# The last four tiles' norms and queries of layer 1 made in rounds of its blocks, and the first gate chain in steps within the feed-forward

## The chip, the cores and the metric

The kernel runs on one core of a Trainium2 chip. The metric is device time in microseconds (us), the median of the runs shown. The engines are named as in the profile: PE is TensorE (PEld its weight loads), DVE is VectorE, ACT is ScalarE, POOL is GpSimd, SP is the queue from which most transfers are issued.

## The reference

Two layers run on 2048 rows of 512 numbers; each layer is an attention over a fixed context and a feed-forward, each with a residual. The part that matters here is the end of layer 0 and the beginning of layer 1:

```python
# layer 0, feed-forward: every activation rounded to 8 bits by row, weights to -1, 0, 1
h = silu(bitlinear(n, w1)) * bitlinear(n, w3)          # n = layernorm(x), 1408 columns
x = x + bitlinear(h, w2)
# layer 1, attention (an mLSTM in parallel form), 8 batches of 256 rows, 16 heads of 32
q  = layernorm(x)
ig = concat(q, ctx, ctx) @ Wi + bi                     # gates, one number for each row and head
fg = concat(q, ctx, ctx) @ Wf + bf
F  = cumsum(log_sigmoid(fg))                           # over the 256 rows
log_D[s, t] = F[s] - F[t] + ig[t]                      # for t <= s
D  = exp(log_D - max_t log_D)
C  = (q @ ctx.T) / sqrt(32) * D
h  = C / (max(|sum_t C|, exp(-max_t log_D)) + 1e-6) @ ctx
x  = x + headwise_norm(h) * ln_scale
# layer 1, feed-forward: 32 experts, 4 for each row, and one shared expert
```

## The kernel before, in words

The 2048 rows are 16 tiles of 128 rows (0 to 15), held in SBUF as `g.X`.

**The feed-forward of layer 0** (`layer0_ffn`) is a software pipeline over tiles. For tile i: `ffn_input` normalizes it on ACT (`xn`), `quantize` takes the row maximum on DVE (`am`), rounds on ACT (line 407) and clips on DVE (`xq`, line 408). `xqT` is that tile transposed by a DMA from the SP queue. `hidden` runs 24 products on PE with w1 and w3 (`p`, line 556), in three chunks of columns; each chunk has an ACT instruction (`sg`, the silu) and a DVE instruction (`h`). The 1408 columns are then rounded in the same manner (`am`, ACT line 407, `hq`), and `hqT` is transposed by a DMA. `output` runs 11 products (`py`, line 575), and DVE adds the result to the tile (`x`, line 576). Two tiles' hidden products can be in flight, since `p1` and `p3` have two PSUM buffers each. The order of instructions on each engine is made here by a scheduler, from the order of the program.

Behind the output, `front(i)` takes the tile's mean and variance for layer 1 (`st`, `mv`). For groups of tiles (0 to 3, 4 to 7, 8 to 11, 12 to 14, and 15 alone) DVE computes the inverse square roots (`rsqrt`, lines 88 to 93, dependent instructions on 128x4 numbers) and `nb`. Each tile is then normalized on ACT, transposed on PE (`ft`, line 584) and copied by ACT to `qT` (`turned`). These pieces wait in the list `todo`, from which two are taken in each step.

**The gates** (class `Gates`). `context` and `queries` sum the gates of all rows in one PSUM tile `pg`; `kept(h)` copies half of it to SBUF (`gs`). `chain(h, ...)` is a generator with one `yield` a step: PE sorts the gates (`gates`, line 502), then bias (DVE, 507 and 508), log-sigmoid (ACT, 511 to 513, with table loads), cumulative sum and maximum (DVE, 515 to 519), then six bf16 parts of two rows of numbers (lines 527 and 529, "casts" and "subtractions" below), each sent to DRAM (`parts_d`), and `em`. Half 0 serves batches 0 to 3, half 1 batches 4 to 7. Half 0 needs tiles 0 to 7 alone. Its chain is begun at the last step but two, so that it runs behind the last tiles.

**The attention of layer 1** (`layer1_attention`). First the constants: `left` is cleared on POOL, `right` is filled on DVE (lines 692, 693, 695), and both get rows from `parts_d` by DMA (`values`). Then 32 blocks (8 batches by 4 groups of heads) run in rounds, in an order written by hand on PE, ACT, DVE and POOL. In round n: the decays of block n (`pd` on PE, lines 726 and 727; `xe`, exponentials on ACT, line 731), the weights of block n-1 (`pqk` on PE, `ct` on DVE, line 754), the products of block n-2 (`num`, line 767, and its copy `numT` on ACT, line 775), and `back` of block n-3. `tail` does the norms of a batch later on. From round 3 on each round takes one step of the second gate chain (half 1), whose PSUM tiles come from the tag `pqk`, of two buffers.

Of the kernel before, what the change touches and what calls it, by code (L numbers as in the profile page):

```python
# [19 lines left out]
F32 = mybir.dt.float32  # L20
BF16 = mybir.dt.bfloat16
# [3 lines left out]
AF = mybir.ActivationFunctionType  # L25
ALU = mybir.AluOpType
# [370 lines left out]
def quantize(g, out, tmp, x):  # L397


    nc = g.nc  # L400
    am = g.small.tile([P, 1], F32, tag="am", name="am")
    nc.vector.tensor_reduce(am, x, AX.X, ALU.max, apply_absolute_value=True)
    inv = g.small.tile([P, 1], F32, tag="qi", name="qi")
    nc.vector.tensor_scalar(inv, am, 1e-5, 1.0 / 127.0, ALU.max, ALU.mult)
    sc = g.small.tile([P, 1], F32, tag="qs", name="qs")
    nc.vector.reciprocal(sc, inv)
    nc.scalar.activation(tmp, x, AF.Identity, bias=g.eps["magic"], scale=sc)
    nc.vector.tensor_scalar(out, tmp, MAGIC, 127.0, ALU.subtract, ALU.min)
    return inv


def ffn_input(g, work, i):

    nc = g.nc
    if i in (0, 4):
        of = slice(0, 4) if i == 0 else slice(4, NT)
        nc.scalar.activation(g.rs[:, of], g.mv[:, of, 1], AF.Sqrt, bias=g.eps["ln"])
        nc.vector.reciprocal(g.rs[:, of], g.rs[:, of])
        nc.vector.scalar_tensor_tensor(g.mv[:, of, 0], g.mv[:, of, 0], -1.0, g.rs[:, of], ALU.mult, ALU.mult)
    xn = work.tile([P, D], F32, tag="y", name="xn")  # L420
    nc.scalar.activation(xn, g.X[i], AF.Identity, bias=g.mv[:, i, 0:1], scale=g.rs[:, i : i + 1])
    xq = work.tile([P, D], BF16, tag="xq", name="xq")
    ix = quantize(g, xq, xn, xn)
    s13 = g.fin.tile([P, 2], F32, tag="s13", name="s13", bufs=4)
    nc.vector.tensor_scalar(s13, g.iw[:, :2], ix, None, ALU.mult)
    return xq, s13
# [9 lines left out]
class Gates:  # L436
# [4 lines left out]
    def __init__(self, g, wp):  # L441
# [12 lines left out]
        self.parts = [wp.tile([P, S], BF16, tag=f"part{n}", name=f"part{n}") for n in range(3)]  # L454
# [4 lines left out]
        self.fg, self.af, self.ig, self.F, self.gg, self.M = (row() for _ in range(6))  # L459

# [10 lines left out]
    def context(self, ps):  # L471

        self.pg = ps.tile([P, CH], F32, tag="pg", name="pg", bufs=1)
        for k in range(KD):
            for c in range(NCH):
                self.g.nc.tensor.matmul(
                    self.pg[c * 2 * H1 : (c + 1) * 2 * H1, :], lhsT=self.Wkv[:, k, :], rhs=self.g.ctxT[c][:, k, :],
                    start=k == 0, stop=False,
                )

    def queries(self, chunks, cols=slice(0, CH)):

        for k in range(KD):
            for c in chunks:
                self.g.nc.tensor.matmul(
                    self.pg[c * 2 * H1 : (c + 1) * 2 * H1, cols], lhsT=self.W[:, k, :], rhs=self.g.qT[c][:, k, cols],
                    start=False, stop=k == KD - 1 and cols.stop == CH,
                )

# [4 lines left out]
    def chain(self, h, two, turned):  # L494
# [11 lines left out]
        yield  # L506
        nc.vector.tensor_scalar(fg, both[r, 1], self.bif[r, 1:2], None, ALU.add)
        nc.vector.tensor_scalar(ig, both[r, 0], self.bif[r, 0:1], None, ALU.add)
# [14 lines left out]
        yield  # L523

        for n, rest in enumerate((gg, M)):
            for m, part in enumerate(self.parts):
                nc.vector.tensor_copy(part[r], rest)
                if m < 2:
                    nc.vector.tensor_sub(rest, rest, part[r])
                (nc.sync if n or h else nc.scalar).dma_start(out=g.parts_d[n, m, r], in_=part[r])  # L530
            yield
# [3 lines left out]
        yield  # L535
        em = self.em[:, :, r]
        nc.scalar.activation(em, pm[:, :, r], AF.Exp, scale=-1.0)

# [3 lines left out]
def layer0_ffn(g, tc, gates):  # L542
# [4 lines left out]
    with tc.tile_pool(name="f0work", bufs=2, reuse_waits="tile") as work, tc.tile_pool(name="f0ps", bufs=2, space=PSUM, reuse_waits="tile") as ps:  # L547

        def hidden(i, xqT, s1, s3):
# [15 lines left out]
            ih = quantize(g, hq, h, h)  # L565
            s2 = work.tile([P, 1], F32, tag="s2", name="s2", bufs=4)
            nc.vector.tensor_mul(s2, ih, g.iw[:, 2:3])
            hqT = work.tile([P, NF, P], BF16, tag="hqT", name="hqT", bufs=3)
            nc.sync.dma_start_transpose(out=hqT, in_=hq)
            return hqT, s2  # L570
# [19 lines left out]
        groups = {3: range(4), 7: range(4, 8), 11: range(8, 12), 14: range(12, 15), 15: range(15, 16)}  # L590
        mv = {}
        todo = []

        def front(i):
            if i == 0:
                todo.append(partial(gates.context, ps))
            for first, of in ((of[0], of) for of in groups.values()):
                if i in of:
                    if i == first:
                        mv["now"] = work.tile([P, 4, 2], F32, tag="mv4", name="mv4")  # L600
                    norm_stats(g, mv["now"][:, i - first, :], g.X[i])
            if i in groups:
                of = groups[i]
                m = mv["now"]
                var = work.tile([P, 4], F32, tag="var4", name="var4")
                nc.vector.tensor_scalar(var[:, : len(of)], m[:, : len(of), 1], 1e-5, None, ALU.add)
                *_, rs = rsqrt(g, var[:, : len(of)], len(of))
                nb = work.tile([P, 4], F32, tag="nb4", name="nb4")
                nc.vector.scalar_tensor_tensor(nb[:, : len(of)], m[:, : len(of), 0], -1.0, rs, ALU.mult, ALU.mult)
                for n, t in enumerate(of):  # L610
                    todo.append(partial(turned, t, rs[:, n : n + 1], nb[:, n : n + 1]))
                    if t == 7:
                        todo.append(partial(gates.queries, (0, 1)))
                        todo.append(partial(gates.kept, 0))
                    if t == 11:
                        todo.append(partial(gates.queries, (2,)))
                    if t > 11:
                        todo.append(partial(gates.queries, (3,), slice((t - 12) * P, (t - 11) * P)))
# [3 lines left out]
        for n in range(len(xq), NT + 5):  # L622
            if n >= 5:
                output(n - 5, *hq.pop(n - 5))
            if 0 <= n - 2 < NT:
                hq[n - 2] = hidden(n - 2, *xq.pop(n - 2))
            if n >= 5:
                front(n - 5)
            for _ in range(2):
                if todo:  # L630
                    todo.pop(0)()
            if n < NT:
                xq[n] = ffn_turned(g, *ffn_input(g, work, n))
            if n == NT + 1:
                one = lambda: ps.tile([P, 2, S], F32, tag="ft", name="gates", bufs=1)
                first = gates.chain(0, one, one)
                for _ in range(8):
                    next(first)
        while todo:
            todo.pop(0)()  # L640
        gates.kept(1)
        for _ in first:
            pass
# [31 lines left out]
def layer1_attention(g, tc, gates):  # L675
    nc = g.nc
    with ExitStack() as ctx:
# [10 lines left out]
        for l, r in zip(left, right):  # L688
            nc.gpsimd.memset(l, 0.0)
            nc.gpsimd.memset(l[:KR], 1.0)  # L690
            if r is right[0]:
                nc.vector.tensor_copy(r[:, 0], g.head.unsqueeze(2).to_broadcast([P, HG, S]))
                nc.vector.tensor_copy(r[:, 1:], r[:, :1].to_broadcast([P, KD - 1, HG, S]))
            else:
                nc.vector.tensor_copy(r, right[0])

        with tc.tile_pool(name="a1ps2", bufs=1, space=PSUM, reuse_waits="tile") as ps, tc.tile_pool(name="a1work", bufs=2, reuse_waits="tile") as work:
            def values(b):

                V = []  # L700
                for j in range(2):
                    v = work.tile([P, D], F32, tag=f"raw{j}", name=f"raw{j}")
                    nc.sync.dma_start(out=v, in_=g.vc_d[b * S + j * P : b * S + (j + 1) * P, :])
                    V.append(v)
# [8 lines left out]
                )  # L713
                return V

# [140 lines left out]
            V, hid, xe, ct, num, numT = {0: values(0)}, {}, {}, {}, {}, {}  # L856
# [4 lines left out]
            def tail(n, r0):  # L861
# [41 lines left out]
            second = gates.chain(  # L903
                1, lambda: ps.tile([P, 2, CH], F32, tag="pqk", name="gates", bufs=2)[:, :, :S],
                lambda: ps.tile([P, 2, CH], F32, tag="pqk", name="pmT", bufs=2)[:, :, :P],
            )

            def round_(n):
# [4 lines left out]
                if 0 <= n - 3 < len(blocks):  # L913
                    b, k = blocks[n - 3]
                    if k == 0:
                        hid[b] = work.tile([P, 2, H1, HD1 + 1], F32, tag="hid", name="hid", bufs=3)
                    back(numT.pop(n - 3), hid[b], k)
# [11 lines left out]
                if n >= 3:  # L929
                    next(second, None)  # L930
# [575 lines left out]
```

## Time and profile before

| | |
|---|---|
| median of 5 runs | 1148.17 us (1145.92 to 1153.21) |
| the profiled execution: its time, its span | 1145.78 us, 1144.0 us |
| mean granted clock of PE | 0.971 |
| PE, DVE, ACT, POOL busy, share of the span | 90%, 48%, 36%, 33% |
| feed-forward of layer 0: first and last product with w1 or w3 | 239.0 and 371.0 us |
| attention of layer 1: first decay product, last `numT` | 407.3 and 557.9 us |

Times inside the execution are counted from the start of its span. A timeline line has start, duration, engine, line, operation, `out<-in`, shapes, how many instructions were merged, and in brackets the engine's idle time just before with what ended it. Lines "SPq" are issues of transfers, not the transfers themselves. In a window line the columns are the window, its length, and for PE, PEld, DVE, ACT, POOL the busy time and the number of instructions, then the granted PE clock, the share of the DMA engines and GB/s.

### The profile page before, as it was taken

Reading aid. Unit: us, or ns where it says so; the run is one execution under the profiler, and the core shown is the slowest. Engines: PE = TensorE matmul, PEld = TensorE weight load, DVE = VectorE, ACT = ScalarE, POOL = GpSimd, SP = SyncE. Lnnn points to the kernel's source line nnn. Section 1 sums busy time; section 2 is a strip of 40 time slices with the busy share of each in tenths; the row PEclk is TensorE's granted clock in tenths of the full one; section 3 lists DMA queues with packets and bytes.
Section 4 is the critical chain, followed back from the end, with each engine's and each line's share of the span. In section 5 each row is a group of like instructions: output and inputs, shape, how many; then the busy total and the mean of one; then the engine's idle time right before and its main releaser. Section 6 shows DMA issues by size and latency. Waiting matters only on the chain.

```text
span 1144.0 us, 14676 instructions
## 1 busy us (share of the span) xinstructions
PE 1034.0 (90%) x5222; PEld 617.1 (54%) x5222; DVE 547.2 (48%) x1443; ACT 412.3 (36%) x701; POOL 375.8 (33%) x347
## 2 busy tenths in 40 slices
PE   7989799989899688898898989999999999999994
PEld 5746466534444255555443445555556665667672
DVE  6545645568888636988845951121221211221210
ACT  4445424155675357578541002111122222111111
POOL 0144522220000001354651033444454555444422
PEclk9999899999999799899899989999999999999997
DMA  9786311023323111221022345766777777788872
GB/s 343 262 284 209 125 56 46 5 50 61 61 52 65 41 40 41 66 78 57 37 92 65 138 149 149 184 167 185 179 193 191 196 197 198 211 226 231 221 186 35
DMA packets 100483, 153.65 MB, mean 134 GB/s; under 512 B 38600, under 2 KB 41288, under 8 KB 100376
## 3 DMA queue, kind: packets, MB, share of 16 engines
q1 hardware_dynamic: 81488, 106.94, 30.2%
q0 software_dynamic: 18672, 45.58, 18.1%
q8 instruction: 43, 0.70, 0.3%
q14 instruction: 40, 0.33, 0.1%
q10 hardware_dynamic: 240, 0.10, 0.0%
HBM read 111.24 MB, written 33.49 MB: 127 GB/s over the span
## 4 chain that ended last, share of the span: by engine, by line
PE 55%; DMA 12%; DVE 11%; issue 7%; ACT 6%; POOL 6%; SPq 0%; POOLq 0%; DVEq 0%; ACTq 0%
PE po L1270 10%; PE pg L1254 9%; PE pu L1254 8%; PE p L556 3%; PE pz L371 3%; PE pw L316 3%; DMA xg<-h_d,tok_of 3%; DMA out_x<-eo,to 2%; POOL out_x L1314 2%; DMA hqT<-hq 2%; PE pt L1310 2%; DMA vc_d<-raw 2%; DMA raw<-in_ctx 2%; DVE xT L1311 2%; ACT xe L731 1%
## 5 line engine op out<-in xcount | busy, mean ns | idle before, releaser
L1314 POOL DMA_INDIRECT out_x<-eo,to x84 | 129.8, 1545 | 226.5 <-ACT eo L1340 211.6
L1254 PE MATMUL pg<-xT,w 128*128 128x288 f32 (+7 forms) x512 | 140.3, 417 | 3.9 <-DVE xT L1311 3.9
L1270 PE MATMUL po<-w,act 128*128 128x512 f32 (+3 forms) x448 | 139.4, 494 | 4.1 <-DVE act L1259 3.8
L1254 PE MATMUL pu<-xT,w 128*128 128x288 f32 (+7 forms) x512 | 136.7, 410 | 0.0
L1258 ACT ACTIVATE sg<-pg 128x288 f32<-128x288 f32 (+8 forms) x68 | 28.9, 425 | 257.6 <-PE pg L1254 254.1
L1340 ACT ACTIVATE eo<-po,slotw 128x512 f32<-128x512 f32 (+3 forms) x112 | 64.2, 578 | 158.8 <-PE po L1270 156.5
L1254 PEld LDWEIGHTS pg<-xT,w 128*128 128x128 f32 x512 | 95.4, 191 | 33.8 <-DVE xT L1311 7.3
L1254 PEld LDWEIGHTS pu<-xT,w 128*128 128x128 f32 x512 | 97.2, 190 | 29.1 <-issue 3.0
L1311 DVE COPY xT<-pt 128x512 f32<-128x512 f32 (+3 forms) x84 | 48.9, 619 | 132.2 <-PE pt L1310 132.1
L1305 DVE SCALAR_TENSOR_TENSOR of<-xg,is_rank 128x32 f32<-128x32 f32 (+3 forms) x84 | 15.8, 188 | 187.2 <-DMA xg<-h_d,tok_of 186.0
L1295 POOL DMA_INDIRECT xg<-h_d,tok_of x84 | 82.6, 983 | 65.0 <-DVE act L1259 37.1
L1270 PEld LDWEIGHTS po<-w,act 128*128 128x128 f32 (+3 forms) x448 | 55.7, 161 | 79.2 <-issue 49.4
L556 PE MATMUL p<-wq,xqT 128*128 128x512 bf16 (+1 forms) x384 | 79.7, 362 | 2.7 <-DMA xqT<-xq 1.9
L754 DVE SCALAR_TENSOR_TENSOR ct<-pqk,xe 128x768 f32<-128x768 f32 x64 | 58.3, 950 | 26.6 <-ACT xe L731 12.9
L316 PE MATMUL pw<-wg,xnT 128*128 128x512 f32 x128 | 60.6, 618 | 0.0
L556 PEld LDWEIGHTS <-xqT 128*128 128x128 bf16 x384 | 36.7, 98 | 44.1 <-DMA xqT<-xq 6.3
L371 PE MATMUL pz<-wo,wyT 128*128 128x512 f32 x128 | 57.9, 595 | 1.5 <-ACT wyT L365 1.5
L1310 PE MATMUL pt<-ident,xg 128*128 128x128 f32 (+4 forms) x336 | 46.1, 269 | 11.7 <-DVE xT L1311 11.7
L731 ACT ACTIVATE xe<-pd 128x512 f32<-128x512 f32 x96 | 54.0, 598 | 5.4 <-PE pd L727 5.0
L1259 DVE TENSOR_TENSOR act<-pu,sg 128x288 f32<-128x288 f32 (+8 forms) x68 | 32.1, 475 | 44.4 <-PE pu L1254 44.1
L1310 PEld LDWEIGHTS pt<-ident,xg 128*128 128x128 f32 (+4 forms) x336 | 35.0, 140 | 31.4 <-DVE xT L1311 16.5
L812 POOL TENSOR_TENSOR hid<-hid,rsq 128x1024 f32<-128x1024 f32 x8 | 15.3, 1913 | 105.5 <-PE pqk L750 79.3
(287 smaller groups left out, 1707.7 us busy)
## 6 DMA issues: line engine op xcount, KB each, us to landing
w<-in_w SPq DMA_DIRECT2D x32, 1024.0 KB
w<-in_w SPq DMA_DIRECT2D x32, 512.0 KB
wst<-in_w1T SPq DMA_DIRECT2D x8, 704.0 KB
wst<-in_w3T SPq DMA_DIRECT2D x8, 704.0 KB
wst<-in_w2T SPq DMA_DIRECT2D x6, 768.0 KB
x<-in_x SPq DMA_DIRECT2D x16, 256.0 KB
ctxT<-in_ctxT_d SPq DMA_DIRECT2D x4, 1024.0 KB
raw<-in_ctx SPq DMA_DIRECT2D x16, 256.0 KB
```

What stands on the lines that cost most here:

```text
L316: nc.tensor.matmul(pw, lhsT=xnT[c][:, k, o : o + P], rhs=wg[:, k, :], start=k == 0, stop=k == KD - 1)
L371: nc.tensor.matmul(pz, lhsT=wyT[:, k, :], rhs=wo[:, k, :], start=k == 0, stop=k == KD - 1)
L556: nc.tensor.matmul(pp[:, : z - a], lhsT=xqT[:, k, :], rhs=w[:, k, a:z], start=k == 0, stop=k == KD - 1)
L731: nc.scalar.activation(out, pd, AF.Exp)
L754: nc.vector.scalar_tensor_tensor(ct[:, r : r + 2, :], pqk[:, :, : S + P], 1.0 / math.sqrt(HD1), xe[:, r : r + 2, :], ALU.mult, ALU.mult,)
L1254: nc.tensor.matmul(pp[:, :n], lhsT=w[:, k, cols], rhs=xT[:, k, :n], start=k == 0, stop=k == KD - 1)
L1270: nc.tensor.matmul(po[h * n : (h + 1) * n, :cols], lhsT=act[:, m, j * P : j * P + n], rhs=w[:, m, h * cols : (h + 1) * cols], start=m == 0 ...
L1295: nc.gpsimd.indirect_dma_start(out=xg[:n], out_offset=None, in_=h_d, in_offset=bass.IndirectOffsetOnAxis(ap=g.tok_of[:n, r, j : j + 1], ax ...
L1310: nc.tensor.transpose(pt[:, k, :n], xg[:n, k * P : (k + 1) * P], g.ident[:n, :n])
L1311: nc.vector.tensor_copy(xT, pt[:, :, :n])
L1314: return nc.gpsimd.indirect_dma_start(out=g.out, out_offset=bass.IndirectOffsetOnAxis(ap=rows, axis=0), in_=eo, in_offset=None, compute_op ...
L1340: nc.scalar.activation(eo[:n, at : at + cols], po, AF.Copy, scale=w[:n, j : j + 1])
```

## The change

Tiles 12 to 15 are no longer normalized, transposed and multiplied into the gates at the end of the feed-forward. Their means and variances go to a tile that outlives it (`gates.last`), one set of inverse square roots for all four is made at the start of `layer1_attention` (`norm_scales`), and the function `extra` puts the rest in rounds: `yn` (ACT) in rounds 1 and 2, transposes and `qT` in rounds 2 and 3, the products of chunk 3 with the gate weights in round 4, added to `gs` by DVE.

The first gate chain is taken in steps, two at each of the last three steps of the feed-forward; what is left of it (`em`) falls in rounds 2 and 3. The two bias instructions are on ACT instead of DVE, and the parts have buffers of their own. The second chain begins at round 6 instead of 3, with the PSUM tag `dec` instead of `pqk`. `todo` gives three pieces a step instead of two. For the last four tiles of the feed-forward the order on PE, ACT and DVE is written out: outputs 12, hidden 15 up to the rounding on ACT, outputs 13 and 14 with their statistics, what `todo` still has, then `hq` of tile 15, and output 15. Two of the three copies that fill `right` are on ACT, and `values` issues `left` and `right` ahead of `raw`.

```diff
@@ quantize
-    nc.vector.tensor_scalar(out, tmp, MAGIC, 127.0, ALU.subtract, ALU.min)
-    return inv
+    return inv, lambda: nc.vector.tensor_scalar(out, tmp, MAGIC, 127.0, ALU.subtract, ALU.min)
...
@@ Gates
+    def added(self, pg):
+        rows = slice((NCH - 1) * 2 * H1, NCH * 2 * H1)
+        self.g.nc.vector.tensor_add(self.gs[rows], self.gs[rows], pg[rows])
...
-        yield
-        nc.vector.tensor_scalar(fg, both[r, 1], self.bif[r, 1:2], None, ALU.add)
-        nc.vector.tensor_scalar(ig, both[r, 0], self.bif[r, 0:1], None, ALU.add)
+        nc.scalar.activation(fg, both[r, 1], AF.Identity, bias=self.bif[r, 1:2])
+        nc.scalar.activation(ig, both[r, 0], AF.Identity, bias=self.bif[r, 0:1])
         yield
...
-            for m, part in enumerate(self.parts):
+            for m, part in enumerate(self.parts[n]):
                 nc.vector.tensor_copy(part[r], rest)
                 if m < 2:
                     nc.vector.tensor_sub(rest, rest, part[r])
-                (nc.sync if n or h else nc.scalar).dma_start(out=g.parts_d[n, m, r], in_=part[r])
+                nc.sync.dma_start(out=g.parts_d[n, m, r], in_=part[r])
...
@@ layer0_ffn, hidden
+            yield
+            end()
             nc.sync.dma_start_transpose(out=hqT, in_=hq)
-            return hqT, s2
+            yield hqT, s2
...
@@ layer0_ffn, the steps
+        gates.first = gates.chain(0, one, lambda: gates.turned_in())
+        for n in range(len(xq), NT + 1):
             if n >= 5:
                 output(n - 5, *hq.pop(n - 5))
+            if n >= 2:
+                *_, hq[n - 2] = hidden(n - 2, *xq.pop(n - 2))
             if n >= 5:
                 front(n - 5)
+                for _ in range(3):
+                    if todo:
+                        todo.pop(0)()
+            if n >= NT - 2:
+                for _ in range(2):
+                    next(gates.first)
             if n < NT:
                 xq[n] = ffn_turned(g, *ffn_input(g, work, n))
-            if n == NT + 1:
-                one = lambda: ps.tile([P, 2, S], F32, tag="ft", name="gates", bufs=1)
-                first = gates.chain(0, one, one)
-                for _ in range(8):
-                    next(first)
-        while todo:
-            todo.pop(0)()
-        gates.kept(1)
-        for _ in first:
-            pass
+        with tc.manual_schedule(engines={E_.PE, E_.Activation, E_.DVE}):
+            i = NT - 4
+            output(i, *hq.pop(i))
+            last = hidden(NT - 1, *xq.pop(NT - 1))
+            next(last)
+            front(i)
+            for i in (NT - 3, NT - 2):
+                output(i, *hq.pop(i))
+                front(i)
+            while todo:
+                todo.pop(0)()
+            hq[NT - 1] = next(last)
+            gates.kept(1)
+            output(NT - 1, *hq.pop(NT - 1))
+            front(NT - 1)
...
@@ layer1_attention
-                nc.vector.tensor_copy(r[:, 0], g.head.unsqueeze(2).to_broadcast([P, HG, S]))
-                nc.vector.tensor_copy(r[:, 1:], r[:, :1].to_broadcast([P, KD - 1, HG, S]))
+                nc.scalar.copy(r[:, 0], g.head.unsqueeze(2).to_broadcast([P, HG, S]))
+                nc.scalar.copy(r[:, 1:], r[:, :1].to_broadcast([P, KD - 1, HG, S]))
             else:
                 nc.vector.tensor_copy(r, right[0])
...
+            def one():
+                return ps.tile([P, CH], F32, tag="dec", name="gates", bufs=2).rearrange("p (n s) -> p n s", n=2)
+            second = gates.chain(1, one, gates.turned_in)
+            rs4, nb4 = norm_scales(g, gates.last)
+            def extra(n):
+                for i in (2 * n - 2, 2 * n - 1):
+                    if 0 <= i < 4:
+                        xn = queries[i]
+                        nc.scalar.activation(
+                            xn, g.X[NT - 4 + i], AF.Identity, bias=nb4[:, i : i + 1], scale=rs4[:, i : i + 1]
+                        )
+                        queries[i + 2] = normed_tile()
+                for i in (2 * n - 4, 2 * n - 3):
+                    if 0 <= i < 4:
+                        turned(NT - 4 + i, queries.pop(i))
+                if n == 4:
+                    pg = ps.tile([P, CH], F32, tag="dec", name="pg", bufs=2)
+                    gates.queries((NCH - 1,), pg)
+                    gates.added(pg)
+                if n in (2, 3):
+                    next(gates.first, None)
+                if n >= 6:
+                    next(second, None)
...
-                if n >= 3:
-                    next(second, None)
+                extra(n)
```

## The prediction

> **What bounds the kernel now.** I read the page first, then the windows around the seam between the two layers, then the timeline there, engine by engine.
>
> ```profile
> PE 1034.0 (90%) x5222; PEld 617.1 (54%) x5222; DVE 547.2 (48%) x1443; ACT 412.3 (36%) x701; POOL 375.8 (33%) x347
> ```
>
> PE is busy for 90% of the span; what PE waits for is what can be won. The windows show where that is:
>
> ```profile
> 340.00:360.00 20.00, 20.00 (x99) 8.66 (x98) 16.69 (x41) 11.17 (x15) 0.00 (x0) 1.00 0.27 50
> 360.00:380.00 20.00, 18.76 (x93) 9.09 (x92) 15.60 (x40) 13.08 (x19) 3.62 (x4) 1.00 0.34 61
> 380.00:400.00 20.00, 8.89 (x35) 4.17 (x34) 14.09 (x51) 5.72 (x8) 0.00 (x0) 0.69 0.14 33
> 400.00:420.00 20.00, 16.64 (x150) 10.25 (x149) 6.39 (x8) 11.69 (x21) 0.00 (x0) 0.97 0.11 39
> ```
>
> From 380 to 400 PE works 8.9 of 20 us: the target of the change. But from 340 to 380, where the first gate chain is moved, PE is full and DVE stands at 16 of 20. PE's own timeline of the seam:
>
> ```profile
> 376.52 1.91 PE L502 MATMUL gates<-sw 64*64 64x256 f32 x8
> 378.36 3.62 PE L485 MATMUL pg<-qT,Wif 128*32 128x512 f32 x8
> 381.91 3.63 PE L575 MATMUL py<-wq,hqT 128*128 128x512 bf16 x16
> 395.98 1.11 PE L584 MATMUL ft<-ident,xn 128*128 128x128 f32 x4 [10.43 <-ACT xn L581]
> 407.31 0.39 PE L726 MATMUL pd<-right,left 128*128 128x512 bf16 x1
> ```
>
> The last `py` ends at 385.54, and the first decay product starts at 407.31: 21.8 us with 10.4 us of nothing and four slow trips through ACT, PE and the gates. I cut the stretch in three. A: up to the end of the last product with w1 and w3 (371.33; 370.68 + 0.65). B: from there to the first `pd` (407.31, so 35.98 us). C: from there to the `numT` of round 13 (473.07, so 65.76 us). Layer 1's experts follow unchanged.
>
> **A: the feed-forward with the chain in it.** The new order on each engine is known from the built program; the durations are those of before.
>
> Three pieces a step put two `xn` (1.51), a rounding (0.80), a `qT` (0.58) and another `xn` (0.83) ahead of the second `sg` of tile 11 on ACT: 3.1 us later (334.0 to 337.1). PE makes most of it good, since the `pg` products move ahead; hidden 12 with `pg` ends at about 349.0, against 347.98: +1.0. Then PE does `gates` (1.91), to 350.9. ACT's queue is strict, and the next thing PE needs from it is `sg` of tile 13:
>
> ```profile
> 348.12 1.56 ACT L407 ACTIVATE h<-h,eps_magic,qs 128x1408 f32<-128x1408 f32 x1 [2.68 <-DVE qs L406]
> 349.59 0.80 ACT L407 ACTIVATE xn<-xn,eps_magic,qs 128x512 f32<-128x512 f32 x1
> 351.42 0.69 ACT L560 ACTIVATE sg<-p,s 128x512 f32<-128x512 f32 x1 [1.03 <-PE p L556]
> 379.41 1.28 ACT L512 ACT_TABLE_LOAD   x1
> 381.14 1.28 ACT L513 ACT_TABLE_LOAD   x1
> 382.44 0.51 ACT L513 ACTIVATE sw<-sw,ones 64x256 f32<-64x256 f32 x1
> ```
>
> In front of it now stand two biases (0.47 each, as lines 507 and 508 take on DVE), absolute value and exponential (0.42 each), a load before the exponential, the rounding of tile 12 (1.56), a load, the logarithm (0.51), the rounding of tile 14 (0.80) and a load back to the silu: 4.7 + 3 x 1.28 = 8.5 us. `sg` starts at 359.4 instead of 351.42. The cover is `py` of tile 10 (2.5), 16 products of tile 13 (3.3) and 7 `py` (1.6), that is until 358.3; then the third chunk waits for the PSUM buffer that this `sg` frees. With the two `sg`-`h` links the products of tile 14 start at 363.1 instead of 357.43: +5.7.
>
> On DVE the chain adds, ahead of the `xq` of tile 15, 0.41, 0.68, 0.42, 0.67, 0.28, 0.41, and 0.28, 0.41, 0.28: 3.8 us. `xq` ends near 370.7 (361.97 before), its transposed copy lands as before some 3.9 us after (361.97 to 365.88), and tile 15's products start at 374.5 (365.88): +8.6, with PE idle for about 4 us, since tile 14 and `py` 12 end at 370.5. The last 2.4 us of casts and subtractions precede the `h` of tile 15, whose first chunk holds PE's last four products: the end moves from 371.33 to about 380.1. A = +8.8. Bounds: +5 (only `gates` and the ACT queue count, the DVE steps find gaps), +11 (all of it, and a cold PE).
>
> A rule that speaks against this: the Trainium skill, "TensorE: Matmul & The Clock Gate", section "HAM oscillation — how this bites in real kernels", wants no PE gaps above about 3.4 us. The rows first: after 5.0 us of waiting, PE took 1.67 us for six products that take some 0.74 us elsewhere:
>
> ```profile
> 460.22 1.67 PE L746 MATMUL pqk<-qT,ctxT 32*128 32x256 f32 x6 [5.00 <-DVE ct L754]
> ```
>
> Such a slow stretch lasted there from 460.2 to 466.4 and cost about 2.3 us. By the rule the new 4 us gap costs the same; I leave it to the range's end here, because DVE sets the pace of tile 15.
>
> Of the ACT loads the Trainium skill, "ScalarE: Activation LUTs", section "Table sets: the hidden batching unit", says that exponential and logarithm share a set and a load takes about 2.7 us. The rows show two loads, 1.28 us each. By the page it would be two loads of 2.7 here instead of three of 1.28, an estimate 1.6 us longer.
>
> **B: to the first decay product.** Counted from the end of tile 15's products. DVE ends `h` at 1.4, `am` (1.62), the scale: 3.5. ACT has three `xn` and a `qT` in front, so the rounding ends at 5.3. `hq` no longer follows it at once: in the written order it stands behind tile 14's statistics, and those behind `py` 14, whose 11 products have two transposes among them, each behind a `qT` on ACT. `py` 14 ends at 7.4; `x` 0.75, `st` 0.69 and 0.18, and `hq` runs from 9.1 to 10.0 (before: 376.12, that is 4.8). The transposed copy lands 3.6 later (as 300.39 to 304.07), at 13.6; the gate products (3.62) end at 12.3 and hide most of that. `py` 15: 2.5, to 16.1. DVE: `x` and statistics to 17.8, 13 dependent instructions at 0.2 (as 384.94, 385.14, 385.34) to 20.4, the copy of `right` 1.22 to 21.7. Only then SP may send rows into `right`, since that copy reads it. Its time to land is not shown; between 1.5 and 3.6 us (no row shorter; the transposes take 3.6); I take 2.8, near the transposes, because it is as small. First `pd` at 24.5 instead of 35.98. B = -11.5; bounds -14 to -9. The ACT copies into `right` (about 1.1 and 2.9 by the slope of line 407's two sizes) start at 8.6 and end at 12.6, hidden by `py` 15.
>
> **C: the rounds.** Two `yn` in round 1: +0.9 beyond ACT's gap. Round 2: two transposes (0.6 each), behind them on ACT two `yn` (0.8 each, which wait for the same transposes), two `qT` (0.58), and PE's next `pd` waits for the PSUM buffers that these free: round 3 begins at 12.5 instead of 8.0 after the first `pd` (415.34 - 407.31): +4.5 so far, the 0.9 included. Round 3: transposes and `qT`, 1.4 more. Round 4: `pg`, 3.6. Sum 9.5. Against it: the second chain in the tag `pqk` cost round 3 a `gates` (1.9) and round 4 a wait for PSUM (3.1), 5.0; in `dec`, at round 6, `gates` 1.9 and the biases on ACT 0.6, so 2.5. Its table loads cost the same, about 4.3, one round later. Its parts: before, 9.2 us in rounds 11 and 12 beyond their 3.4 each, since casts and subtractions ran under POOL:
>
> ```profile
> 455.45 1.15 DVE L527 CAST part<-sw 64x256 bf16<-64x256 f32 x1
> 461.16 0.29 DVE L527 CAST part<-sw 64x256 bf16<-64x256 f32 x1
> ```
>
> One step further back in the chain, scan and sum meet POOL instead and most casts come behind it; by the same rows about 5.7. So C = 9.5 - 5.0 + 2.5 - 3.5 = +3.5. Bounds 0 (ACT's order hides the round trips) and +8 (parts as dear as before, one more slow stretch).
>
> **Sum.** 8.8 - 11.5 + 3.5 = +0.8; for the two new idle gaps (4 us before tile 15, 8 us before the first `pd`) I add 1.5, part of twice 2.3. +2.3 on 1145.78 is 1148.1. The profiled execution is 2.4 below the median of the runs: 1150.5 us.
>
> **Rivals.** The forecast (chance 0.5): gained and lost are nearly equal, 1145 to 1156.
> Faster (0.2): the feed-forward absorbs the chain, A = +3, because ACT's third load and DVE's steps fall in waits that are there anyway; then B counts nearly whole: -5 to -9 us, 1142 near the middle. For it: ACT has 11 of 20 us busy. Against: the queue is in order, and the loads stand ahead of `sg`. It decides if tile 15's products start before 370.
> Slower (0.3): ACT's round trips between transposes and `qT` in rounds 2 to 4 are the new wait, each with a PE that has gone cold: C = +8, A = +10, 1157 to 1160. It decides from a third round that starts over 14 us after the first `pd`.
> That the change doesn't do what it says is partly so already in the forecast: `right` still waits for the last tile's norms on DVE, so the seam shrinks and doesn't close.
>
> **Numbers.** Half a per cent, 5.7 us, is about what a measurement of this kernel can tell from no change. Below -5.7 lies most of the faster case, with some of it inside: 0.16. Above +5.7 lies the slower case and a little of the forecast: 0.34. Inside: 0.5. For 8 in 10 I take A and C at their ends in part: -9 to +11 around the median before, 1139.5 to 1160; the likeliest case alone is 1145 to 1156.
>
> **What the profile after would show.** Right: table loads between 351 and 360 and a late `sg`; tile 15's first product after an idle gap near 374; `py` 15 ending near 396; first `pd` near 404.5, after the DVE copy of `right`; slow rounds 2 to 4. Wrong: a feed-forward that ends within 4 us of before, a first `pd` before 400, or rounds 2 to 4 of 3.4 us each.

## The result, and the profile after

The changed kernel takes 1151.34 us (median of 52 runs, 1142.34 to 1156.78) against 1148.38 us before (94 runs, 1140.61 to 1157.34). The ratio is 1.0025, with a 95% interval of 1.0014 to 1.0036: slower by about 3 us, where the forecast had 2.3 us (1150.5 against the 1148.17 known then). The profiled execution took 1148.61 us, its span is 1146.8 us, its mean granted clock 0.967.

First the busy times and the windows of the changed kernel, in the columns of the view shown before:

```profile
PE 1036.6 (90%) x5198; PEld 614.3 (54%) x5198; DVE 541.2 (47%) x1425; ACT 419.4 (37%) x708; POOL 376.6 (33%) x347
```

```profile
340.00:360.00 20.00, 18.77 (x87) 8.00 (x86) 15.46 (x35) 15.37 (x21) 0.00 (x0) 1.00 0.23 44
360.00:380.00 20.00, 15.89 (x70) 7.17 (x70) 17.64 (x50) 8.69 (x12) 0.19 (x1) 0.91 0.31 59
380.00:400.00 20.00, 13.50 (x60) 5.52 (x57) 12.24 (x35) 11.91 (x13) 3.43 (x4) 0.96 0.23 60
400.00:420.00 20.00, 13.93 (x121) 7.71 (x122) 5.71 (x7) 11.38 (x21) 0.00 (x0) 0.78 0.07 18
```

From 380 to 400 PE works 13.5 us instead of 8.9: the seam has indeed been filled. But from 340 to 380, where PE lacked 1.2 us of 40 before, it now lacks 5.3, and from 400 to 420 it works 2.7 us less than before. The list of PE's waits between 340 and 480 us (line waiting, releaser, total us, times, longest) says for what:

```profile
PE pd L750 <- DMA right<-parts_d: 7.8, 1, 7.8
PE pqk L770 <- DVE ct L778: 3.8, 2, 2.3
PE p L562 <- DMA xqT<-xq: 3.5, 1, 3.5
PE back L806 <- ACT numT L799: 2.6, 1, 2.6
PE pd L750 <- ACT xe L755: 1.9, 2, 1.2
PE gates L540 <- ACT qT L874: 1.7, 1, 1.7
PE p L562 <- ACT sg L566: 1.5, 1, 1.5
```

The wait of 10.4 us for the last tile's `xn` is gone. In its place stand 7.8 us for the rows of `right`, 3.5 us for tile 15's input, 1.7 us for a `qT` in the rounds. PE's own timeline has them in order; the number in brackets is the idle time just before:

```profile
360.26 0.81 PE L562 MATMUL p<-wq,xqT 128*128 128x384 bf16 x4 [1.49 <-ACT sg L566]
373.72 6.61 PE L562 MATMUL p<-wq,xqT 128*128 128x512 bf16 x24 [3.48 <-DMA xqT<-xq]
393.11 2.55 PE L583 MATMUL py<-wq,hqT 128*128 128x512 bf16 x11 [1.40 <-DMA hqT<-hq]
403.44 0.58 PE L750 MATMUL pd<-right,left 128*128 128x512 bf16 x1 [7.78 <-DMA right<-parts_d]
415.83 0.34 PE L540 MATMUL gates<-ident,sw 64*128 64x64 f32 x2 [1.70 <-ACT qT L874]
```

And ACT's and DVE's, at the three table loads in the feed-forward and at the copy of `right` that ends the seam:

```profile
352.52 1.28 ACT L519 ACT_TABLE_LOAD   x1
355.70 1.28 ACT L520 ACT_TABLE_LOAD   x1
358.23 1.28 ACT L566 ACT_TABLE_LOAD   x1
359.52 1.27 ACT L566 ACTIVATE sg<-p,s 128x512 f32<-128x512 f32 x2
```

```profile
399.81 0.16 DVE L660 SCALAR_TENSOR_TENSOR nb<-last,rsq 128x4 f32<-128x4 f32 x1
399.89 1.22 DVE L713 COPY right<-right 128x4096 bf16<-128x4096 bf16 x1
```

In the three stretches of the prediction, with the profiled executions side by side:

| stretch | before | after | difference | forecast |
|---|---|---|---|---|
| A: to the end of the last product with w1 or w3 | 371.33 | 380.33 | +9.0 | +8.8 |
| B: from there to the first `pd` | 35.98 | 23.11 | -12.9 | -11.5 |
| C: from there to `numT` of round 13 | 65.76 | 72.34 | +6.6 | +3.5 |
| added for the new idle gaps | | within A and C | | +1.5 |
| to round 13 | | | +2.7 | +2.3 |
| round 13 to the last `numT` | 84.79 | 87.86 | +3.1 | 0 |
| from there to the end of the span | 586.1 | 583.2 | -2.9 | 0 |

The last two rows are no part of the change: but for the end of the second chain the code is the same there, and in the twelve profiles of this study the first of them takes 83.5 to 87.9 us and the second 581.4 to 588.6. PE's stretches at half clock come in some profiles and not in others: from 8 to 12 us after the `numT` of round 13 the granted clock was 0.57 in four of the twelve and 1.00 in the other eight. A single profile can therefore place a microsecond in a stretch, but the sum of a change of 3 us is told only by the repeated runs.

### The profile page after: what moved, and what is told of

Its sections match the earlier page's. It is cut to its first block, busy times and chain, and to the rows that moved or that the text cites. A ratio compares the mean times of both kernels' runs of the same rounds, so it can differ in the third digit from the quotient of the medians.

```text
span 1146.8 us, 14612 instructions
## 1 busy us (share of the span) xinstructions
PE 1036.6 (90%) x5198; PEld 614.3 (54%) x5198; DVE 541.2 (47%) x1425; ACT 419.4 (37%) x708; POOL 376.6 (33%) x347
## 4 chain that ended last, share of the span: by engine, by line
PE 38%; DVE 7%; issue 6%; ACT 4%; DMA 4%; POOL 4%; POOLq 0%; DVEq 0%; ACTq 0%; SPq 0%
PE po L1320 10%; PE pg L1304 9%; PE pu L1304 8%; DMA out_x<-eo,to 2%; POOL out_x L1364 2%; PE pt L1360 2%; DVE xT L1361 2%; DMA xg<-h_d,tok_of 1%; PE po L1019 1%; ACT xe L755 1%; PE num L791 1%; PE pqk L770 1%; DVE ct L778 1%; PE pd L750 1%; PE pgu L999 1%
## 5 line engine op out<-in xcount | busy, mean ns | idle before, releaser
L755 ACT ACTIVATE xe<-pd 128x512 f32<-128x512 f32 x96 | 54.5, 599 | 17.7 <-PE pd L751 17.3
L583 PE MATMUL py<-wq,hqT 128*128 128x512 bf16 x176 | 43.2, 380 | 8.6 <-DMA hqT<-hq 8.6
```

The source lines that it names most:

```text
L755: nc.scalar.activation(out, pd, AF.Exp)
```

## The experiments

Each kernel was timed beside the kernel before on the same chip; "ratio" is to that. The medians were taken on different chips: the kernel before had 1149.63 us beside chain_late, dve_late, hq_early and right_apart, 1146.07 beside no_extra, second_later, kept_warm and best, and 1147.85 beside the last two. So kernels are compared here by their ratios, and an expected time is held against the ratio times 1148.38. The three stretches are read from one profiled execution of each kernel. As the start of the feed-forward itself moves by some 3 us from one profile to the next, its length is counted from its own first product with w1 or w3.

| kernel | median us | ratio, 95% interval | feed-forward | its end to first `pd` | first `pd` to `numT` of round 13 |
|---|---|---|---|---|---|
| before | 1148.38 | 1 | 132.3 | 36.0 | 65.8 |
| changed | 1151.34 | 1.0025 (1.0014 to 1.0036) | 140.6 | 23.1 | 72.3 |
| chain_late | 1151.49 | 1.0026 (1.0004 to 1.0048) | 134.4 | 30.5 | 73.0 |
| dve_late | 1155.57 | 1.0071 (1.0036 to 1.0106) | 141.4 | 29.6 | 73.1 |
| hq_early | 1149.04 | 1.0001 (0.9975 to 1.0027) | 140.7 | 21.6 | 73.4 |
| right_apart | 1146.13 | 0.9970 (0.9943 to 0.9998) | 138.8 | 16.8 | 72.1 |
| no_extra | 1140.65 | 0.9944 (0.9916 to 0.9972) | 141.2 | 23.0 | 63.9 |
| second_later | 1147.50 | 0.9990 (0.9959 to 1.0022) | 132.5 | 39.6 | 63.3 |
| kept_warm | 1150.18 | 1.0028 (0.9999 to 1.0058) | 141.1 | 24.9 | 72.7 |
| best | 1141.10 | 0.9955 (0.9932 to 0.9978) | 134.3 | 19.1 | 72.7 |
| yn_four | 1146.21 | 0.9984 (0.9958 to 1.0009) | 140.6 | 23.3 | 72.0 |
| best_yn_four | 1136.77 | 0.9902 (0.9869 to 0.9936) | 135.3 | 18.4 | 70.4 |

**A: what lengthens the feed-forward.** The first kernel takes the whole chain out of it, the second only its DVE half.

```diff
@@ chain_late: steps of the feed-forward
-            if n >= NT - 2:
-                for _ in range(2):
-                    next(gates.first)
@@ the pieces of tiles 8 to 11: all in the written order
-                for _ in range(3):
+                for _ in range(3 if n < NT else 0):
@@ the written order
             output(i, *hq.pop(i))
-            last = hidden(NT - 1, *xq.pop(NT - 1))
+            next(gates.first)
+            last = hidden(NT - 1, *xq.pop(NT - 1), mid=lambda: next(gates.first))   # mid: behind the sg
             next(last)
             front(i)
+            for _ in range(4):
+                next(gates.first)
```

> The first gate chain leaves the feed-forward: its gates stand on PE in front of tile 15's products, its exponential and logarithm on ACT behind tile 15's three sg, its DVE instructions behind the row maximum of tile 15; the last four of the waiting pieces go to the written order too. All else is as in the changed kernel. If the chain in ACT's and DVE's queues is what made the feed-forward longer (my theory), the last product with w1 or w3 ends at 371 to 374 us instead of 380.3. Behind it DVE now has the chain (6 us) ahead of hq of tile 15, so the first pd comes 27 to 30 us later, at 399 to 403 instead of 403.4: 1147 to 1151 us in all. If three pieces a step or the order written by hand made it longer (rival), the products end at 378 or later and the first pd at 406 to 410: 1154 to 1158 us.

The feed-forward takes 134.4 us, 6.2 less than in the changed kernel, and 2.1 more than before, about the 1.9 us of `gates` on PE. (The absolute end, 377.26, lies outside the expected 371 to 374 because the feed-forward began 3.1 us later than in the changed kernel, at 242.87.) So three pieces a step and the written order cost nothing here that shows; the chain does. What was won in A was lost behind it: 30.5 us to the first `pd` (27 to 30 were expected), because the chain now stands there, and the time is that of the changed kernel.

```diff
@@ dve_late
-            if n >= NT - 2:
+            if n == NT - 2:
                 for _ in range(2):
                     next(gates.first)
@@ the written order
             next(last)
+            for _ in range(4):
+                next(gates.first)
             front(i)
```

> Only the first two steps of the chain (gates, biases, absolute value, exponential, logarithm with their table loads on ACT) stay in the feed-forward, at the step where they are now; the four steps on DVE come behind the row maximum of tile 15. This parts the two halves of A. If ACT's queue gives +5.7 and DVE's steps the rest (my theory), the last product with w1 or w3 ends at 376 to 378 us. If ACT alone sets it, 380; if DVE alone, 372 to 373. Behind it hq of tile 15 waits 4 us longer for DVE: the first pd at 403 to 406, 1151 to 1155 us.

The DVE steps are gone from the feed-forward, and it is no shorter: 141.4 us. My split was wrong. The rounding and the clip that make tile 15's input show it, first in the changed kernel, then in this one:

```profile
368.40 0.80 ACT L407 ACTIVATE xn<-xn,eps_magic,qs 128x512 f32<-128x512 f32 x1
369.39 0.41 DVE L408 TENSOR_SCALAR xq<-xn 128x512 bf16<-128x512 f32 x1
```

```profile
367.83 0.80 ACT L407 ACTIVATE xn<-xn,eps_magic,qs 128x512 f32<-128x512 f32 x1
368.77 0.42 DVE L408 TENSOR_SCALAR xq<-xn 128x512 bf16<-128x512 f32 x1
```

The same clip before, and the row maximum of tile 13 on DVE, which stands ahead of it:

```profile
355.98 1.62 DVE L402 TENSOR_REDUCE am<-h 128x1 f32<-128x1408 f32 x1
361.55 0.42 DVE L408 TENSOR_SCALAR xq<-xn 128x512 bf16<-128x512 f32 x1
```

Counted from the start of the feed-forward (239.76 and 239.18) both clip at 129.6 us; before, it was 122.5 (361.55 - 239.04). So DVE's nine steps delay the input by nothing that can be seen, not by 2.9 us, and ACT's queue by all of the 7.1: counted in the same way, the first `sg` of tile 13 starts 7.4 us later than before (359.52 and 351.42 in the two profiles), and that row maximum 7.2 us later (363.91 and 355.98).

What was moved came back behind the feed-forward, and dearer than expected: the chain on DVE stands ahead of `hq` of tile 15, its `py` starts 17.7 us after the last product with w1 or w3 instead of 12.8, and the first `pd` came at 410.2 instead of the expected 403 to 406. The ratio, 1.0071, is that of some 1156.5 us, above the expected 1151 to 1155.

**B: what holds the first decay product.**

```diff
@@ hq_early: the written order
             next(last)
+            hq[NT - 1] = next(last)
             front(i)
...
-            hq[NT - 1] = next(last)
```

> hq of tile 15 is taken on DVE, and its transpose sent, right behind the rounding on ACT instead of behind the outputs 13 and 14 and the waiting pieces. My theory: it starts 4 us earlier on DVE, but PE has the pg products in front of py 15 until 391.7, so py 15 comes 1.4 us earlier and so does the first pd (402.0): 1149.5 to 1150.5 us. Rival: the place of hq is what keeps py 15 back, py 15 at 389 and the first pd at 399.5: 1147.

The end of the feed-forward to the first `pd` is 1.5 us shorter, as expected: `py` 15 follows the `pg` products at once, and no earlier. (The ratio, 1.0001, is lower than the changed kernel's 1.0025, but its interval takes that in.)

```diff
@@ right_apart: filling right of the odd batches
-                nc.vector.tensor_copy(r, right[0])
+                nc.vector.tensor_copy(r[:, 0], g.head.unsqueeze(2).to_broadcast([P, HG, S]))
+                nc.vector.tensor_copy(r[:, 1:], r[:, :1].to_broadcast([P, KD - 1, HG, S]))
```

> right of the odd batches is filled from head by two instructions on DVE instead of being copied from right of the even batches; so the transfer into the first right no longer waits for a copy that DVE takes only behind the last tile's norms. If that copy is what holds the first pd (my theory), pd follows py 15 at 395.7 to 397 instead of 403.4, and PE, which no longer stands idle for 7.8 us, takes the first two rounds 1.5 to 2 us faster; the yn of round 1 then wait for the norms' scales (nb at 402), which takes back 1 to 3 us: 1143 to 1147 us. If the rows of left or raw, or ACT's table load, are as late as the copy (rival), the first pd stays at 402 to 403.5 and the time at 1150 to 1152.

```profile
373.26 4.93 PE L562 MATMUL p<-wq,xqT 128*128 128x512 bf16 x23 [3.47 <-DMA xqT<-xq]
390.94 2.55 PE L583 MATMUL py<-wq,hqT 128*128 128x512 bf16 x11 [1.39 <-DMA hqT<-hq]
394.94 0.38 PE L751 MATMUL pd<-right,left 128*128 128x512 bf16 x1 [1.45 <-DMA right<-parts_d]
```

PE waits 1.45 us for the rows of `right` instead of 7.78, and B goes from 23.1 to 16.8 us. The rows themselves were ready long before: what they waited for was a copy that only reads `right`, behind the norms of the last tile on DVE. This one edit makes the changed kernel faster than the one before, at a ratio of 0.997 whose interval ends just under 1.

The feed-forward, whose code is that of the changed kernel, is 1.8 us shorter in this profile. That is the clock and not the edit: tile 15's products ran at full speed (4.93 us, granted clock 1.00 from 373 to 378), behind the same wait that they follow in the changed kernel, where they took 6.61 us. This profiled execution is also the fastest of the runs of right_apart, 1136.39 us against a median of 1146.13.

**C: the price of the rounds.**

```diff
@@ no_extra: before the rounds
-            queries = {i: normed_tile() for i in range(2)}
+            queries = {}
+            nc.gpsimd.memset(qT[NCH - 1], 0.0)
@@ extra(n)
-                    if 0 <= i < 4:          # yn, and transposes with qT
+                    if 0 <= i < 0:
...
-                if n == 4:                  # the products of chunk 3 with the gate weights
+                if n == -4:
```

> The changed kernel without what it put in rounds 1 to 4 for the last four tiles: no yn, no transposes, no qT copies and no chunk-3 products with the gate weights (their queries are left at zero and their part of the gates is left out). It gives the price of that work in C. By the forecast's step it is 9.5 us: from the first pd to numT of round 13 some 63 us instead of 72.3, and 1141 to 1143 us in all. If C is longer because of a slow PE clock or the later second chain (rival), most of the 72.3 us stays: 69 or more, and 1148 to 1151.

63.9 us instead of 72.3: the work put in the rounds costs 8.4 us there, and the whole kernel is 0.8% shorter without it (0.9944 against 1.0025). The rival, that most of the length of C comes from a slow clock or the second chain, falls. The rest of C, without that work, is 1.8 us shorter than before (63.9 against 65.8). Its first three rounds took 1.4 us more than before (9.45 against 8.04), behind the wait for `right` and at half clock at first (granted clock 0.50 from 404 to 408); from round 3 on, where the second chain is, it is 3.2 us shorter.

```diff
@@ second_later: the kernel before
+            def one():
+                return ps.tile([P, CH], F32, tag="dec", name="gates", bufs=2).rearrange("p (n s) -> p n s", n=2)
-            second = gates.chain(1, <tiles of the tag pqk>)
+            second = gates.chain(1, one, lambda: one()[:, :, :P])
...
-                if n >= 3:
+                if n >= 6:
                     next(second, None)
@@ chain, for h == 1: the biases on ACT, no step between the sums and the parts
```

> The kernel before with one part of the change alone: the second gate chain starts in round 6 instead of 3, takes its PSUM tiles from the tag of the decays instead of pqk, and has its two biases on ACT. By the forecast's steps it saves 5.0 and 3.5 us and costs 2.5: the stretch from the first pd to numT of round 13 is 6 us shorter than the 65.8 of before, 1142 us. Read off the rounds of the changed kernel's trace (gates 1.9, the step with the table loads 1.9, the parts -2, no wait for PSUM -5) it is 3 us: 1145. If the stalls only move with the chain (rival), 65 to 67 us and 1147 to 1150.

63.3 us instead of 65.8. The 2.5 us hold a loss that is not the second chain's: in this profile the four trips through `ft` and `pg` in the seam ran at half clock throughout (granted clock 0.50 from 396 to 414), where before the clock was 1.00 from 402 on; the seam was 3.6 us longer, and rounds 0 to 2, in which the second chain has no step, took 1.2 us more (9.27 against 8.04). From round 3 on the later chain saves 3.7 us, somewhat more than the 3 read off the trace and far from the forecast's 6. By rounds, against before: 5.4 less in rounds 3 and 4, 3.5 more in rounds 5 to 8, 1.9 less from round 9 on. In the whole time it is not to be told from no change.

```diff
@@ yn_four
             queries = {i: normed_tile() for i in range(2)}
+            both = work.tile(shape, F32, tag="sq", name="yn2", bufs=1).rearrange("p h d -> p (h d)")
+            queries[2], queries[3] = both[:, :D], both[:, D:]
...
-                        queries[i + 2] = normed_tile()
```

> The changed kernel with buffers of their own for the yn of tiles 14 and 15 (the tile sq, which is free until round 8), so that these two no longer wait for the transposes of tiles 12 and 13 to read the two yn buffers, and run in the 1.7 us in which ACT waits for those. If the order yn, qT on ACT is what lengthens round 2 (my step for C), PE's wait of 1.70 us for qT in front of the third round goes to 0.2 us, the first pd to numT of round 13 takes 70.5 to 71 us instead of 72.3, and the time is 1149 to 1150 us. If another wait or the slow clock takes its place (rival), 72 to 73 us and 1151.

```profile
417.63 0.33 PE L540 MATMUL gates<-ident,sw 64*128 64x64 f32 x2 [0.24 <-ACT qT L874]
```

PE's wait goes from 1.70 to 0.24 us, and the first `numT` comes 11.5 us after the first `pd` (418.17 - 406.66) instead of 12.9 (416.38 - 403.44). That the wait was ACT's order is shown. Its worth is less clear: up to round 13 only 0.3 of these 1.4 us are left in this profile, since rounds 5 to 13 took 1.1 us more than in the changed kernel, while the ratio is 0.4% lower than the changed kernel's (0.9984 against 1.0025, and the intervals do not meet), more than the wait explains. Where the rest comes from was not settled.

**The clock.**

```diff
@@ kept_warm: behind output(NT - 1) and its statistics
+            for _ in range(14):
+                pt = ps.tile([P, KD, P], F32, tag="ft", name="warm", bufs=1)
+                for k in range(KD):
+                    nc.tensor.transpose(pt[:, k, :], g.ident, g.ident)
```

> The changed kernel with 56 transposes of the unit matrix on PE, read by nobody, behind py 15, in the 7.8 us in which PE waits for right. If PE is slow in the first rounds because it stood idle (my 1.5 us for the new gaps), the 12 decay products of the first two rounds take 0.38 and 0.27 us each instead of 0.6 and 0.42, the first numT comes 11 to 11.5 us after the first pd instead of 12.9, and the time is 1.5 to 2 us less: 1149 to 1150. If the slow clock has another cause, or the rounds wait for ACT anyway (rival), 1151 as before.

```profile
396.29 9.90 PE L655 MATMUL warm<-ident 128*128 128x128 f32 x56
406.03 0.38 PE L754 MATMUL pd<-right,left 128*128 128x512 bf16 x1
418.77 0.45 PE L754 MATMUL pd<-right,left 128*128 128x512 bf16 x1
419.01 0.63 PE L755 MATMUL pd<-lateb,identb 128*128 128x512 bf16 x1
419.57 1.25 PE L774 MATMUL pqk<-qT,ctxT 32*128 32x256 f32 x8
```

Half of it came as expected: with the gap filled, `pd` takes 0.38 us from the first on, and the first `numT` comes 11.6 us after it (417.66 - 406.03). But 56 transposes took 9.9 us, not 7, and so put off the first `pd` by some 2 us; and a slow stretch came all the same, in round 3, behind the 1.70 us wait for `qT`. C is 72.7 us, and the ratio, 1.0028, is that of the changed kernel. The slow clock is real, but moving it is no gain; PE has to have work.

**Put together.** `best` has the chain behind the feed-forward, `hq` of tile 15 in the middle of it, `py` 15 ahead of the last `pg`, two `xn` of tiles 8 to 11 in flight, and `right` of the odd batches filled apart, in round 0; `best_yn_four` has the edit of yn_four as well.

```diff
@@ best: the written order (product is output without its sum on DVE, normal is turned up to xn)
             output(i, *hq.pop(i))
+            next(gates.first)
             front(i)
             last = hidden(NT - 1, *xq.pop(NT - 1), mid=lambda: next(gates.first))
             next(last)
+            for i in (8, 9):
+                tile[i] = todo.pop(0)()
+            for i in (13, 14):
+                add[i] = product(i, *hq.pop(i))
+            for _ in range(2):
+                next(gates.first)
             hq[15] = next(last)
+            next(gates.first)
+            add[13]()
+            next(gates.first)
...          # the other turned pieces and statistics, py 15, pg of chunk 2, kept(1)
@@ right of the odd batches: filled from head by DVE, in round 0
```

> What the runs so far point to, put together: the first chain's gates on PE behind py 12 and ahead of tile 15's products, its exponential and logarithm on ACT behind the last sg, its DVE steps behind tile 15's row maximum, hq of tile 15 between them; xn and qT of tiles 8 to 11 behind it in a written order, two in flight; py 15 ahead of the last pg; right of the odd batches filled from head. If ACT's queue is what lengthened the feed-forward and the copy of right what held the first pd, the last product with w1 or w3 ends 2 us later than before (372 to 375) and the first pd comes 16 to 19 us behind it, at 389 to 393 instead of 403.4: 1136 to 1141 us. If the chain behind the products only makes ACT late there (rival), the first pd is at 396 or later: 1144 or more, no better than right_apart.

> The same edit in the kernel best: first pd at 389 to 391 us, 1.5 us less in the rounds: 1138.5 to 1140 us. Rival: no less than best, 1141.

Lines of PE's timeline of `best`, from the gates ahead of the last tile's products to the first `pd`:

```profile
363.42 1.94 PE L510 MATMUL gates<-sw 64*64 64x256 f32 x8
365.29 4.93 PE L562 MATMUL p<-wq,xqT 128*128 128x512 bf16 x23
382.59 3.20 PE L585 MATMUL py<-wq,hqT 128*128 128x512 bf16 x9 [0.22 <-issue]
385.72 3.62 PE L489 MATMUL pg<-qT,Wif 128*32 128x512 f32 x8
389.28 0.39 PE L771 MATMUL pd<-right,left 128*128 128x512 bf16 x1
```

Tile 15 no longer waits behind an ACT queue with table loads in it, `pd` follows `pg` without any wait, and it runs at full clock. The seam is 19.1 us, at the upper end of the expected 16 to 19, with a feed-forward only 2.0 us longer than before. `best` is faster than before, but by less than expected: the ratio, 0.9955, is that of 1143.2 us, where 1136 to 1141 were expected and the rival had 1144 or more. `best_yn_four` is faster than expected: 0.9902, interval 0.9869 to 0.9936, that is 1137.1 us, on six runs. It beats both kernels. Why one edit of two buffers should give 0.5% more (the intervals of the two just overlap), when C is 2.3 us shorter, no run shows. Of the rest, C costs it 4.6 us against before.

## Why the prediction was right, and where it was not

The time (1150.5 forecast, 1151.34 measured) and the sum to round 13 (+2.3 forecast, +2.7 measured in the profile) agree, and so does the kind of outcome: what the seam gains, the feed-forward and the rounds take back. That the number is so close is in part luck: C came out 3.1 us dearer than its sum, and B, 1.4 us better, with the 1.5 us set aside for a cold PE covered nearly all of that. Step by step:

- **A, the size, right** (+8.8 forecast; +9.0 in the profile, of which 0.7 is a later start). The three table loads fell at 352.5, 355.7 and 358.2; `sg` of tile 13 started at 359.5 (forecast 359.4), the products of tile 14 at 362.95 (363.1), those of tile 15 at 373.72 (374.5), behind a wait of 3.48 us (4).
- **A, the reason for its second half, wrong.** The step "On DVE the chain adds, ahead of the `xq` of tile 15 ... 3.8 us" carried 2.9 us of the sum. dve_late shows none of it. I had counted the late `sg` by what it does to the products of tile 14, 5.7 us, since PE had other work to fill some of it. But tile 15's input hangs on the same `sg` through DVE's row maximum, and there all 7 us arrive. And 1.7 us of A is the clock, which I had kept for the range's end: 24 products took 6.61 us where tile 14's took 4.92. So the size of A is partly luck: it holds a slow clock in place of the DVE steps, and in right_apart, where the clock stayed full, A is 1.8 us shorter.
- **B, right in each step** and 1.4 us better. Counted from the end of the products: `hq` at 8.3 (forecast 9.1), its transposed copy 12.8 (13.6), `py` 15 done 15.3 (16.1), the copy of `right` done 20.8 (21.7); the rows then landed in 2.3 us (2.8). right_apart shows that the DVE copy is what decides, as said.
- **C, right in kind, mis-sized in two terms of the second chain.** The round trips were forecast at 9.5 and cost 8.4 (no_extra). The third round started 12.9 us after the first `pd` (12.5), and `pg` in round 4 took 3.6. The second chain was to save 6.0 (5.0 - 2.5 + 3.5); from round 3 on it saves 3.2 (no_extra) to 3.7 (second_later). The 5.0 in rounds 3 and 4 came (5.4 in both). The loads that were to "cost the same" did not: with `gates` and the biases, 2.5 forecast, rounds 5 to 8 took 3.3 (no_extra) and 3.5 us (second_later) more than before. And the parts, -3.5 forecast, gave less: rounds 11 and 12 together took 14.1 us in the changed kernel where before they took 16.1 (from `pd` to `pd`: 456.93 to 471.04, and 453.45 to 469.50), so -1.9, and with rounds 9, 10 and 13, into which the slow stretch now reaches, -1.5 (-1.2 and -1.9 in the two other kernels). POOL did hit the steps further back in the chain, as expected, and most casts got away:

```profile
456.80 2.29 DVE L526 TENSOR_TENSOR_SCAN sw<-sw 64x256 f32<-64x256 f32 x1
461.39 1.34 DVE L528 TENSOR_TENSOR sw<-sw 64x256 f32<-64x256 f32 x1
462.77 1.16 DVE L529 TENSOR_SCALAR sw<-sw 64x256 f32<-64x256 f32 x1
466.74 1.67 PE L770 MATMUL pqk<-qT,ctxT 32*128 32x256 f32 x6 [2.33 <-DVE ct L778]
```

  The scan takes 2.29 us there, 0.68 in the feed-forward (line 526 at 359.74). That puts off `ct`, PE waits twice, and behind the second wait the clock is slow again (six `pqk` in 1.67 us, as before). The waits for DVE were shortened, from 5.00 us to 1.43 and 2.33; the slow stretch behind them was not (460.2 to 466.4 before, 466.7 to 473.6 now).
- **The 1.5 us for cold PE** went where I put it, behind the waits ahead of tile 15 and of the first `pd`, and was too small: 1.7 us in A, and in C some 1.4 in the first rounds (by no_extra), whose granted clock was 0.59 from 403 to 410 in the changed kernel.
- **The rivals.** "Faster" was to decide by tile 15 starting before 370: it started at 373.7. "Slower" by a third round over 14 us after the first `pd`: 12.9. That `right` still waits for the last norms was seen, but as a remark; it cost 6.3 us, and an edit of two lines cures it.

On the rule weighed in A: in the changed kernel PE had no work for 7.78 us, and from 403 to 410 the granted clock was 0.59. That agrees with the Trainium skill, "TensorE: Matmul & The Clock Gate", section "HAM oscillation — how this bites in real kernels", which warns of gaps above some 3.4 us. At that size and below it the runs disagree with one another. Behind the wait ahead of tile 15 the products ran slow in the changed kernel (3.48 us, granted clock 0.74 from 373.7 to 380.3) and at full speed in right_apart (3.47 us). And in kept_warm a wait of 1.70 us, after three shorter ones (1.6 us together) in the 10 us ahead of it, was followed by products at half speed (0.63 us for a `pd` at 419.01 that takes 0.38), as it was in hq_early and best, while the same wait in the changed kernel was not, nor in right_apart, where one of 1.78 us stood 5 us ahead of it. Two windows behind it, the changed kernel first, then kept_warm:

```profile
418.00:420.00 2.00, 2.00 (x36) 1.51 (x36) 0.95 (x2) 0.71 (x2) 0.00 (x0) 1.00 0.05 16
420.00:422.00 2.00, 2.00 (x24) 1.24 (x24) 0.66 (x1) 0.28 (x1) 0.00 (x0) 0.50 0.08 25
```

The measurement decides: from 1.7 to 3.5 us the length of a wait does not tell whether the slow clock follows. What does was not settled.

## What to carry to other kernels

Work moved beside a full engine is not hidden by the engines that have time left: an in-order queue with table loads in it holds back the next instruction that the full engine needs, and everything that hangs on that. Follow the delayed instruction to all its readers, not only to the next one on the bound engine; the later reader may have no slack. And when a transfer comes late, look at who reads its target: a copy that reads the destination can hold it as surely as its source.

## What was not expected of the hardware

- The 56 transposes of kept_warm took 9.90 us, 0.177 each, and not 7. In the trace they start 0.11 to 0.17 us apart within a group of four, as in the groups elsewhere, and 0.33 us apart from one group to the next. All groups write one PSUM tile (`bufs=1`); whether that is the reason was not tested.
- Stretches at half clock come and go where the code is all but the same: from round 13 to the last `numT` the twelve profiles range from 83.5 to 87.9 us. What sets off one there was not settled.
